# Deformable samples of a fused two-layer block: windows of 16 by 8 against two 8 by 8 patches on the halves of the array

## The chip, the cores and the metric

The kernel runs on one core of one Trainium2 chip, in float32 throughout, as one launch. The metric is device time in microseconds of that core. Five engines work side by side, each in its own order: TensorE (PE, its weight loads PEld), VectorE (DVE), ScalarE (ACT), GpSimd (POOL) and SyncE (SP), which here only issues transfers. Semaphores tie them together. Transfers run on 16 DMA engines.

## The reference, cut to what matters

Two layers act on x of 32 images, 128 channels, 32 by 32 points; each adds its result to its input, after a group norm of it. Layer 0 is a long convolution over the 1,024 points in 1,024 inner channels, with a GLU, a layer norm and a decoder. Layer 1 is a deformable depthwise convolution with 64 taps (8 by 8), and it is the one that the change touches:

```python
off = depthwise_conv3x3(x, offset_w) + offset_b      # 2 * 64 channels: dx, dy of each tap
for tap in range(64):                                # at each of the 32*32 points
    ix = (gx + kx[tap] + off[tap, 0]) * W / (W - 1) - 0.5
    iy = (gy + ky[tap] + off[tap, 1]) * H / (H - 1) - 0.5
    s = bilinear(x, iy, ix)                          # 4 neighbours, zero outside the image
    acc += s * weight[:, tap]
out = gelu(batch_norm(acc))
```

The offsets are the same for all channels, so a bilinear sample of all 128 channels is a matrix product: pixels of the image (rows) times weights of those pixels (columns). The weight of a pixel is a product of two hat functions, max(0, 1 - |ix - px|) and max(0, 1 - |iy - py|).

## The kernel before

The first stage (`ssm_kernel_table`, `ssm_convolution`) makes the convolution's result y for all images and leaves it in DRAM. `main_block` does the rest. Its order is written out by hand: Python generators yield the cost of what they have just issued, and `run_along` always advances the one that is least far along by its own total.

**first_part(b)** is the GLU of image b: two halves of 512 points, eight blocks m each, with eight products for the gate (L785), eight for the value (L808), one for the encoder (L824) and one for the decoder (L713), 128 rows by 512 columns; two more close a half. That is 292 products an image.

**second_part(b)** is layer 1 of image b. It runs beside `first_part(b + 2)`, so images 30 and 31 have no GLU beside them. The columns u = x + kx (39 of them) are grouped in 17 `PACKS`; a pack holds all (u, kx) pairs, called slots, whose samples lie in one window 8 pixels wide: 8 to 16 slots a pack, 254 in all. A pack is worked in four pieces of two ky each. A piece has 128 rows, the pixels of a window of 16 rows by 8, and a column for each slot, ky and output row y, up to 1,024. The y of a column decides in which of three windows (`YWINDOWS`, rows 0, 8 or 16 on) its sample lies, so a piece is three products (L1119), with `rows_of` giving the stretches of y. Each is scaled from PSUM by the tap's weight into `prod` (L1122, DVE). GpSimd adds the piece's two ky (L1139) and then adds them to the accumulator, u by u (L1144).

The moving operand of those products is made of two tables in DRAM for each image, `hat_d0` of 8 x hats and `hat_d1` of 16 y hats. For each piece `load_hat` loads them with repeats, the x hats into `ds` and the y hats into `dhy` (L1057, SyncE), and `weights(k)` multiplies the one by the other on DVE (L1076). `ds` has SB = 5 buffers and is loaded five pieces ahead; `dhy` has HB = 4 and is loaded four pieces ahead of its multiplication. A load is split into one for each run of neighbouring slots: one for most packs, two or four for the packs at the image's edges (25 runs a piece index over all packs, so 200 loads an image). The window of pixels comes with three loads of 128 runs of 512 bytes for each new x0 (L1090). In images 30 and 31 (`ALONE`) a quarter of `ds` is loaded and copied on (L1068).

**prepare(b + 1)** runs inside `second_part(b)`, as steps with due times on a scale of 204 an image: group norm, nine tap operations for the offsets, the transposed image to DRAM, then the positions `rel` (L934, L945), a `spread` of them to `rel_d` in DRAM with 16 copies of 256 runs of 128 bytes (L952), a `gather` back into two tiles (L966), and 24 hats: two ScalarE operations of 624 columns (L981, L982) and a write of 312 KB (L983) each, in two buffers. Image 0 is prepared in `opening`, beside `first_part(1)`:

```python
run_along((first_part(1), FIRST), (opening(), 90.0))
...
run_along(
    (first_part(b + 2, last=(b + 2 == B - 1)), FIRST),
    (second_part(b, steps), SECOND),
)
```

SyncE issues, in one order, the loads of `ds`, `dhy`, windows, y and u and the copies of `spread`; the writes of hats go out on ScalarE's queue. In the built program each of these transfers also waits for the one eight before it, since they share eight semaphores in turn. `deformable_redo` behind it repeats an image with a general method if its largest offset passes a bound (`BOUND_X`, `BOUND_Y`).

Of the kernel before, what the change touches and what calls it, by code (L numbers as in the profile page):

```python
# [515 lines left out]
KY2 = 2  # L516
SLOT = KY2 * H
PIECES = 8 // KY2
NPIECE = NU * 8 * SLOT
NCOL = PIECES * NPIECE  # L520
# [8 lines left out]
YWINDOWS = (0, 8, 16)  # L529
BOUND_X, BOUND_Y = 2.45, 3.25  # L530
# [9 lines left out]
def rows_of(piece):  # L540

    a, b = 15 - KY2 * piece, 23 - KY2 * piece
    return (0, a), (a, b - a), (b, H - b)
# [30 lines left out]
def main_block(nc, tc, const, ins, x, u_d, y_d, x1_d, out, offmax):  # L574
# [18 lines left out]
    ALONE = B - 2  # L593
    SB, HB = 5, 4
    ctx = ExitStack()
    with ctx:
# [5 lines left out]
        one, two, three = pool("mb1", 1), pool("mb2", 2), pool("mb3", 3)  # L602
        spool, hypool, hatpool = pool("mbs", SB), pool("mbh", HB), pool("mbq", 2)
        ppool = pool("mbp", 3)
# [34 lines left out]
        minus = constant("minus", [P, 16])  # L639
# [32 lines left out]
        rel_d = []  # L672
        zero = hatpool.tile([P, HSUB], F32, tag="hat", name="zero")
        nc.gpsimd.memset(zero, 0.0)
        for i in range(2):
            t = dram1.tile([2, NCOL], F32, tag=f"rel_d{i}", name=f"rel_d{i}")
            flat = t.rearrange("a (p l) -> (a p) l", p=P // 2)
            n = 2 * NCOL // P
            for lo in range(0, n, HSUB):
                w = min(HSUB, n - lo)  # L680
                nc.sync.dma_start(flat[:, lo : lo + w], zero[:, :w])
            rel_d.append(t)

# [177 lines left out]
        def prepare(b):  # L861
# [85 lines left out]
            def spread(a):  # L947
                def run():
                    for ky in range(8):

                        g = a * 8 + ky
                        nc.sync.dma_start(  # L952
                            at(
                                rel_d[b % 2],
                                a * NCOL + ky // KY2 * NPIECE + 7 * SLOT + ky % KY2 * H,
                                [[7 * SLOT, 8], [8 * SLOT, W], [1, H]],
                            ),
                            st["rel"][g * 8 : (g + 1) * 8],
                        )

                return run

            def gather(a):
                def run():
                    t = st["t", a] = one.tile([P, HSUB], F32, tag=f"rel{a}", name=f"dr_{b}_{a}")
                    nc.sync.dma_start(  # L966
                        t, at(rel_d[b % 2], a * NCOL, [[HSUB, P], [1, HSUB]])
# [4 lines left out]
            def hat(a, k):  # L972


                def run():
                    if k == 0:
                        st[f"h{a}"] = dram.tile(
                            [(8, 16)[a], NCOL], F32, tag=f"hat_d{a}", name=f"dhat_{b}_{a}"
# [5 lines left out]
                        at(st[f"h{a}"], k * NCOL, [[HSUB, P], [1, HSUB]]), t  # L984
# [4 lines left out]
            hats = [hat(0, k) for k in range(8)] + [hat(1, k) for k in range(16)]  # L989

            def turn(n):


                def run():
# [7 lines left out]
                    if n == 1:  # L1002
# [3 lines left out]
                        )  # L1006

                return run

            def ready():  # L1010
                images[b] = st["vt_d"], [st["h0"], st["h1"]]
# [5 lines left out]
                (71, largest), (74, across), (79, down), (81, spread(0)), (82, spread(1)),  # L1017
                (89, gather(0)), (90, gather(1)),
                *((96 + 82 * i // len(hats), step) for i, step in enumerate(hats)),
# [24 lines left out]
        def load_hat(k, a):  # L1044
# [4 lines left out]
            hats = images[b][1]  # L1049
            if a == 0:  # L1050
                t = s_of[k] = spool.tile([P, 16, KY2, H], F32, tag="s", name=f"ds_{k}")
            else:
                t = hy_of[k] = hypool.tile([P, 16, KY2, H], F32, tag="hy", name=f"dhy_{k}")
            rows = 4 if a == 0 and b >= ALONE else 16
            for first, slot, m in runs_of(n):
                dims = [[[0, rows], [NCOL, 8]], [[NCOL, rows], [0, 8]]][a]
                nc.sync.dma_start(  # L1057
                    t[: rows * 8, slot : slot + m],
                    at(hats[a], i * NPIECE + first * SLOT, [*dims, [1, m * SLOT]]),
                )  # L1060

        def spread_fine(k):

            if k >= len(pieces) or pieces[k][0] < ALONE:
                return
            m = slots_of(pieces[k][1])
            for n in (32, 64):
                nc.scalar.copy(s_of[k][n : 2 * n, :m], s_of[k][:n, :m])  # L1068
# [10 lines left out]
        def windows(b, n):  # L1079
# [4 lines left out]
            if b == B or (n > 0 and PACKS[n - 1][0] == x0):  # L1084
                return
            t = xw_of[b, x0] = three.tile(
                [P, len(YWINDOWS), C], F32, tag="xw", name=f"dxw_{b}_{x0}"
            )
            for j, y0 in enumerate(YWINDOWS):
                nc.sync.dma_start(  # L1090
                    t[:, j, :],
                    at(images[b][0], (y0 * W + x0) * C, [[W * C, 16], [C, 8], [1, C]]),
                )

        def second_part(b, steps):
# [6 lines left out]
            for n in range(NP):  # L1102
# [3 lines left out]
                windows(b, n + 1)  # L1106
                for i in range(PIECES):
                    k = (b * NP + n) * PIECES + i
                    s = s_of.pop(k)
                    w = wk[:, table_of[n] : table_of[n] + m, KY2 * i : KY2 * (i + 1)]  # L1110
                    prod = ppool.tile([P, 16, KY2, H], F32, tag="prod", name=f"dp_{k}")
                    for j, (y0, ny) in enumerate(rows_of(i)):
                        while steps and steps[0][0] <= 3 * (PIECES * n + i) + j:
                            steps.pop(0)[1]()
                        ps = psam.tile([P, 512], F32, tag="sam", name=f"dps_{k}_{j}")
                        ps = ps[:, : m * KY2 * ny].rearrange(
                            "p (s k y) -> p s k y", s=m, k=KY2
                        )
                        nc.tensor.matmul(  # L1119
                            ps, xw[:, j, :], s[:, :m, :, y0 : y0 + ny], start=True, stop=True  # L1120
                        )
                        nc.vector.tensor_mul(  # L1122
                            prod[:, :m, :, y0 : y0 + ny],
                            ps,
# [221 lines left out]
```

## Time and profile before

| | us |
|---|---|
| median of 3 runs (lowest, highest) | 13420.71 (13418.3, 13433.87) |
| the profiled execution | 13421.61 |
| its span, first to last instruction | 13419.9 |
| first memset of the accumulator (L1101), image 0 | 1827.2 |
| the same, image 30 | 12880.3 |
| the same, image 31 | 13164.7 |

The stage up to about 1,280 us is the long convolution. From there to 1,827 the GLU of images 0 and 1 runs; then 30 periods of one image's samples beside another's GLU; then two images of samples alone. A profile's group line reads: line, engine, operation, tiles written <- read, sizes and count, then busy us and mean ns of one, then how long the engine had idled ahead of such instructions and on whom. A float32 product appears as two PE records, each with a weight load (PEld); a record's end is modelled and overlaps the next one's start, so the cadence is read from start to start.

### The profile page before, as it was taken

What the parts mean: (1) busy time and instruction counts of PE and PEld (TensorE: products, weight loads), DVE (VectorE), ACT (ScalarE), POOL (GpSimd) and SP (SyncE); (2) the same over time, 40 slices, a digit from 0 to 9 for tenths busy, and PEclk for the clock granted to TensorE, in tenths of its full rate; (3) what the DMA queues carried; (4) which work ended last, traced back from release to release, by engine and by line L of the source; (5) the groups of instructions that cost most, each with busy time, mean ns of one, the idle gap of its engine ahead of it and who ended that gap; (6) DMA issues with size and microseconds to landing.
All of it is one profiled execution on the core that took longest, in us unless ns stands there. A gap on an engine that the chain in (4) does not pass through costs nothing.

```text
span 13419.9 us, 133500 instructions
## 1 busy us (share of the span) xinstructions
PE 12998.3 (97%) x40482; PEld 7208.8 (54%) x40482; DVE 8388.1 (63%) x12173; ACT 3279.7 (24%) x4767; POOL 9064.3 (68%) x8871
## 2 busy tenths in 40 slices
PE   7998999999999999999999999999999999999975
PEld 7998445555555555555555555555555555555533
DVE  5554146666666666666666666666666666666677
ACT  4433122222222212112222222211122222221245
POOL 2554147777777777777677777777777777777778
PEclk8999999999999999999999999999999999999988
DMA  7998068888888888888888888888888888888866
GB/s 232 274 284 267 19 172 235 240 235 236 232 230 240 236 228 228 233 231 239 237 237 232 229 239 239 231 225 232 231 240 236 236 232 231 236 240 232 232 194 174
DMA packets 1721768, 3055.43 MB, mean 228 GB/s; under 512 B 445523, under 2 KB 1024467, under 8 KB 1720019
## 3 DMA queue, kind: packets, MB, share of 16 engines
q1 hardware_dynamic: 1508434, 2591.60, 72.0%
q10 hardware_dynamic: 163456, 320.92, 6.6%
q0 software_dynamic: 49152, 134.28, 3.3%
q8 instruction: 328, 5.37, 0.2%
q14 instruction: 398, 3.25, 0.1%
HBM read 2580.03 MB, written 466.06 MB: 227 GB/s over the span
## 4 chain that ended last, share of the span: by engine, by line
PE 86%; DMA 7%; DVE 2%; ACT 2%; issue 1%; POOL 1%; SPq 1%; ACTq 0%; DVEq 0%; POOLq 0%
PE gpg L785 24%; PE gpv L808 24%; PE dps L1119 23%; PE psy L320 5%; DMA ds<-dhat 4%; PE gph L824 3%; PE gpo L713 3%; PE psz L237 3%; DMA dhat<-dh 1%; DVE ds L1076 1%; DMA dhy<-dhat 1%; ACT ds L1068 1%; SPq L1057 0%; DMA u<-u_d 0%; DVE dp L1122 0%
## 5 line engine op out<-in xcount | busy, mean ns | idle before, releaser
L1122 DVE TENSOR_TENSOR dp<-dps,k_weight_slots 128x256 f32<-128x256 f32 (+17 forms) x6528 | 3085.4, 483 | 3084.2 <-PE dps L1119 2908.7
L1119 PE MATMUL dps<-ds,dxw 128*128 128x256 f32 (+18 forms) x13056 | 4698.9, 447 | 227.5 <-DVE ds L1076 185.6
L1144 POOL TENSOR_TENSOR dacc<-dacc,dp 128x256 f32<-128x256 f32 (+3 forms) x4736 | 4403.9, 930 | 398.3 <-DVE dp L1139 28.5
L1119 PEld LDWEIGHTS dps<-ds,dxw 128*128 128x128 f32 x13056 | 2468.8, 192 | 3213.9 <-issue 2543.1
L785 PE MATMUL gpg<-gy,g_w_glu 128*128 128x512 f32 x8192 | 3986.4, 593 | 22.9 <-DMA gy<-y_d 18.2
L808 PE MATMUL gpv<-gy,g_w_glu 128*128 128x512 f32 x8192 | 3974.7, 592 | 0.0
L1139 POOL TENSOR_TENSOR dp<-dp 128x448 f32<-128x448 f32 (+2 forms) x2142 | 2671.9, 1247 | 1898.1 <-DVE dp L1122 1895.4
L1076 DVE TENSOR_TENSOR ds<-ds,dhy 128x1024 f32<-128x1024 f32 (+3 forms) x2176 | 3163.4, 1454 | 783.3 <-DMA ds<-dhat 675.5
L785 PEld LDWEIGHTS gpg<-gy,g_w_glu 128*128 128x128 f32 x8192 | 1544.5, 190 | 1237.0 <-issue 968.4
L808 PEld LDWEIGHTS gpv<-gy,g_w_glu 128*128 128x128 f32 x8192 | 1548.9, 189 | 1157.9 <-issue 915.1
L846 POOL TENSOR_TENSOR gs<-gs,gq 128x512 f32<-128x512 f32 x448 | 633.0, 1413 | 1348.2 <-ACT gq L845 1348.2
L845 ACT ACTIVATE gq<-gr 128x512 f32<-128x512 f32 x448 | 282.2, 630 | 4665.5 <-DVE gr L837 4603.9
L357 POOL DMA_DIRECT2D y_d<-yo x1024 | 589.5, 583 | 694.1 <-ACT yo L344 624.6
L792 ACT ACTIVATE gs<-gpg,k_b_glu 128x512 f32<-128x512 f32 x512 | 351.8, 687 | 2494.1 <-PE gpg L785 2378.0
L981 ACT ACTIVATE dh<-dr,k_minus 128x624 f32<-128x624 f32 x768 | 621.7, 809 | 654.7 <-DMA dhat<-dh 574.2
L320 PE MATMUL psy<-toe,z 128*128 128x192 f32 x4096 | 668.0, 326 | 7.4 <-DVE z L242 5.5
L320 PEld LDWEIGHTS psy<-toe,z 128*128 128x128 f32 x4096 | 663.0, 196 | 11.6 <-DVE z L242 6.8
L816 DVE SCALAR_TENSOR_TENSOR gs<-gpv,k_b_glu,gs 128x512 f32<-128x512 f32 x512 | 379.9, 742 | 437.2 <-PE gpv L808 436.8
L982 ACT ACTIVATE dh<-dh,one 128x624 f32<-128x624 f32 x768 | 626.2, 815 | 25.0
L715 POOL TENSOR_TENSOR gs<-gs,gr 128x512 f32<-128x512 f32 x448 | 631.7, 1410 | 0.0
L824 PE MATMUL gph<-gu,k_W_enc 128*128 128x512 f32 x1024 | 525.9, 595 | 30.1 <-DVE gs L816 30.1
L335 DVE TENSOR_TENSOR psy<-psy,t 128x256 f32<-128x256 f32 (+2 forms) x768 | 333.7, 434 | 346.1 <-ACT t L328 329.3
(163 smaller groups left out, 5810.3 us busy)
## 6 DMA issues: line engine op xcount, KB each, us to landing
dhy<-dhat SPq DMA_DIRECT2D x1536, 512.0 KB
ds<-dhat SPq DMA_DIRECT2D x1440, 512.0 KB
dhat<-dh ACTq DMA_DIRECT2D x768, 312.0 KB
y_d<-yo POOLq DMA_DIRECT2D x1024, 128.0 KB, 4.2
gy<-y_d SPq DMA_DIRECT2D x512, 256.0 KB
u<-u_d SPq DMA_DIRECT2D x224, 512.0 KB
dxw<-dvt_d SPq DMA_DIRECT2D x1248, 64.0 KB
dhy<-dhat SPq DMA_DIRECT2D x256, 224.0 KB
```

Of the source, the lines that this page charges most:

```text
L320: nc.tensor.matmul(ps[:, c // 2, c % 2, :], rows[i][:, (g * CG + c0 + c) // 2, c % 2, :], toe[:, c0 + c, :], start=True, stop=True,)
L715: nc.gpsimd.tensor_add(sums[0], sums[0], r)
L785: nc.tensor.matmul(gate, w_glu[:, k, D + m * P : D + m * P + P], ys[k], start=(k == 0), stop=(k == KD - 1),)
L808: nc.tensor.matmul(val, w_glu[:, k, m * P : m * P + P], ys[k], start=(k == 0), stop=(k == KD - 1),)
L824: nc.tensor.matmul(h, w_enc[:, m * P : (m + 1) * P], u, start=True, stop=True)
L846: nc.gpsimd.tensor_add(sums[1], sums[1], sq)
L982: nc.scalar.activation(t, t, AF.Relu, scale=-1.0, bias=const["one"])
L1076: nc.vector.tensor_mul(s[:, :m], s[:, :m], hy[:, :m])
L1119: nc.tensor.matmul(ps, xw[:, j, :], s[:, :m, :, y0 : y0 + ny], start=True, stop=True)
L1122: nc.vector.tensor_mul(prod[:, :m, :, y0 : y0 + ny], ps, w[:, :, :, None].to_broadcast([P, m, KY2, ny]),)
L1139: adder.tensor_add(prod[:, :m, 0], prod[:, :m, 0], prod[:, :m, 1])
L1144: nc.gpsimd.tensor_add(to, to, prod[:, slot : slot + nj, 0])
```

## The change

A piece is now four products of 64 rows. The rows of the array are two sides of 64, each a patch of 8 by 8 pixels; the columns of a side are 32 cells a slot, up to 512. Side 0 has the low rows v = y + ky, side 1 the high ones. Pieces 1 to 3 have, on each side, four neighbouring v for all eight ky; piece 0 has the rest at the top and bottom. Each side needs two patches (`parts_of`), which start at even rows, so there are two products of 64 rows a side, issued side 0, side 1, side 0, side 1. The sides write two PSUM tiles.

- `ds` and `dhy` tiles are half as wide. `ds` is one load a run as before (16 rows, eight repeats); `dhy` is now two loads of 64 partitions a run, 8 repeats of 8 rows. There are 8 y hats instead of 16, so 16 hats in place of 24.
- Pieces 1 to 3 are scaled by one DVE operation a side, piece 0 by four a side (`blocks_of`): 238 an image in place of 204. They write runs of four (or one) y into `prods`, two tiles of one pack each, laid out by ky.
- GpSimd sums the eight ky of a pack at once (three operations) and then adds to the accumulator, once for each u and pack: 37 additions an image in place of 148.
- The positions go to `rel_n` with two copies (`lay`), and 56 copies from DRAM to DRAM (`spread`) bring them into the order of the cells: 12 of 64 by 39 runs of 4 numbers, 28 of 8 by 39 runs of 1 to 6, and 16 of 8 by 39 single numbers. They are due at 81 to 108, the gathers at 112 and 113, the hats from 118 to 178.
- Patches are laid out in DRAM by 16 copies (`window`), and a pack's patches then come with two loads of 64 partitions for each x0, in two buffers instead of three.
- The special case for the last two images is gone. `BOUND_Y` falls from 3.25 to 2.45.

```diff
-KY2 = 2
-SLOT = KY2 * H
-PIECES = 8 // KY2
-NPIECE = NU * 8 * SLOT
-NCOL = PIECES * NPIECE
+CELLS = 32
+PIECES = 4
+SIDE = PIECES * NU * 8 * CELLS
+NCOL = 2 * SIDE
...
+def parts_of(side, piece):
+
+    if piece == 0:
+        return ((0, 0, 28), (6, 28, 32)) if side == 0 else ((6, 4, 32), (0, 0, 4))
+    w = 2 * (piece - 1) + side
+    return (w, 0, 2), (w + 1, 2, 4)
...
+                def move(to, ky, y, dims):
+                    frm = a * ASTEP + LEAST - 7 * H + ky * KSTEP + y
+                    moves.append(lambda: nc.sync.dma_start(
+                        at(rel_d[b % 2], a * NCOL + to, [[d[1], d[0]] for d in dims]),
+                        at(rel_n[b % 2], frm, [[d[2], d[0]] for d in dims]),
+                    ))
+
+                us = (NU, 8 * CELLS, H)
+                js = (8, CELLS, jump)
+                for side in range(2):
+                    base = side * SIDE
+                    for piece in range(1, PIECES):
+                        move(
+                            base + piece * NU * 8 * CELLS, 0,
+                            FIRST_V[side] + 4 * (piece - 1),
+                            ((64, 4, KSTEP - 1), us, (4, 1, 1)),
                         )
+                    for ky, y, n, cell in edges_of(side):
+                        move(base + cell, ky, y, (js, us, (n, 1, 1)))
+                    for i in range(4):
+                        ky = 4 * side + i
+                        move(
+                            base + (28, 0)[side] + i, ky, 19 - ky, (js, us, (1, 1, 1))
+                        )
...
-                (71, largest), (74, across), (79, down), (81, spread(0)), (82, spread(1)),
-                (89, gather(0)), (90, gather(1)),
-                *((96 + 82 * i // len(hats), step) for i, step in enumerate(hats)),
+                *((54 + i, window(i // 8, i % 8)) for i in range(16)),
+                (68, largest), (70, across), (74, down), (76, lay(0)), (77, lay(1)),
+                *((81 + i // 2, step) for i, step in enumerate(moves)),
+                (112, gather(0)), (113, gather(1)),
+                *((118 + 60 * i // len(hats), step) for i, step in enumerate(hats)),
...
+                if a == 0:
+                    nc.sync.dma_start(
+                        to, at(src, frm, [[SIDE, 16], [0, 8], [1, m * CELLS]])
+                    )
+                else:
+                    for side in range(2):
+                        nc.sync.dma_start(
+                            to[side * 64 : side * 64 + 64],
+                            at(
+                                src, frm + side * 8 * SIDE,
+                                [[0, 8], [SIDE, 8], [1, m * CELLS]],
+                            ),
+                        )
...
+                    for part in range(2):
+                        for side in range(2):
+                            half = slice(64 * side, 64 * side + 64)
+                            w, lo, hi = parts_of(side, i)[part]
+                            to, frm = ps[side], s[half, :m]
...
+                            nc.tensor.matmul(
+                                to[..., lo:hi], xw[half, w, :], frm[..., lo:hi],
+                                start=True, stop=True,
+                            )
+                    yield measure(m)
...
+                    due(1)
+                    scale(0)
+                    yield measure(m)
+                    due(2)
+                    scale(1)
+                    weights(k + 2)
+                    yield measure(m)
                     load_hat(k + SB, 0)
...
+                nc.gpsimd.tensor_add(rows(2, 2, 2), rows(2, 2, 2), rows(0, 6, 2))
+                nc.gpsimd.tensor_add(rows(2, 1, 1), rows(2, 1, 1), rows(4, 1, 1))
+                total = prod[:, 2 * KS : 2 * KS + m * H]
+                nc.gpsimd.tensor_add(total, total, prod[:, 3 * KS : 3 * KS + m * H])
```

In the changed kernel the products stand at L1224, the copies from DRAM to DRAM at L1002, the loads of `ds` at L1144 and of `dhy` at L1149.

## The prediction

> **What bounds the kernel now.** I read the page's busy shares and chain first, then the sums by stretch, then TensorE's and SyncE's order of time in single stretches.
>
> ```profile
> PE 12998.3 (97%) x40482; PEld 7208.8 (54%) x40482; DVE 8388.1 (63%) x12173; ACT 3279.7 (24%) x4767; POOL 9064.3 (68%) x8871
> PE 86%; DMA 7%; DVE 2%; ACT 2%; issue 1%; POOL 1%; SPq 1%; ACTq 0%; DVEq 0%; POOLq 0%
> ```
>
> ```profile
> 1835.00:12865.00 11030.00, 10963.39 (x30084) 5628.83 (x30083) 7142.79 (x10036) 2309.68 (x3061) 7950.49 (x7363) 1.00 0.86 233
> 12880.00:13164.00 284.00, 172.54 (x420) 91.36 (x420) 216.93 (x310) 181.13 (x195) 214.27 (x202) 0.79 0.65 189
> 13165.00:13420.00 255.00, 148.94 (x404) 79.83 (x404) 198.22 (x294) 134.12 (x135) 214.20 (x201) 0.85 0.62 175
> ```
>
> The columns are stretch, length, then busy time of PE, PEld, DVE, ACT and POOL, clock, DMA share, GB/s. The first row holds 30 images: each runs its samples beside another image's GLU (`first_part`). TensorE is busy 99% of it and nothing else over 72% (POOL), but the DMA engines stand at 0.86. The last two rows are images 30 and 31, which have no GLU beside them; there TensorE is not the bound. The accumulator's memsets (L1101) start at 1827.2 and, 30 images later, at 12880.3: 368.4 us an image.
>
> ```profile
> 6003.22 0.97 PE L1119 MATMUL dps<-ds,dxw 128*128 128x480 f32 x2
> 6004.02 1.88 PE L808 MATMUL gpv<-gy,g_w_glu 128*128 128x512 f32 x4
> 6005.74 0.97 PE L1119 MATMUL dps<-ds,dxw 128*128 128x480 f32 x2
> 6006.55 1.88 PE L808 MATMUL gpv<-gy,g_w_glu 128*128 128x512 f32 x4
> 6008.26 0.62 PE L1119 MATMUL dps<-ds,dxw 128*128 128x256 f32 x2
> ```
>
> Each product is two records. From start to start, two GLU products take 1.72 us, so 0.86 each (1.68 ns a column), and 480 sample columns take 0.81. An image has 292 GLU products (251 us) and 254 slots x 8 x 32 = 65,024 sample columns: 109 us, plus 204 products' small extra of 0.03 = 115. With 2 us for transposes and statistics the sum is 368: TensorE's order explains the period with nothing left over.
>
> **Part 1, TensorE.** 204 products of 128 rows become 272 of 64 rows with the same columns in all. If the halves do not work at the same time, that is 109 + 272 x 0.03 = 117 us, no gain. If they do, the order decides: side 0, side 1, side 0, side 1, each with two records, and the second record of a product needs the half that the first one holds. So side 1's first record runs beside side 0's second, and eight record lengths become five: 109 x 5/8 = 68, plus 5 for small extras = 73. Weight loads keep pace: in the first stage 368 records of 128 columns, each with a load ahead, take 41.50 us, 113 ns each; eight make 0.9 us a piece, under five records' 1.0.
>
> ```profile
> 284.70 41.50 PE psz L237 x368
> ```
>
> No row shows the array going from whole to halves. It may cost nothing; or the pipeline empties, at most the tail of a record, 593 - 430 = 163 ns. I take the tail, since it is what a wait for the last column would expose: 136 changes x 0.16 = 22 us. TensorE needs 251 + 2 + 73 + 22 = 348 us an image (326 without the changes; 392 if the halves take turns). The Trainium skill, TensorEngine Tiling (Array Packing), Key Properties, says that tiles run products in parallel and that changing the tiling mode drains TensorE. No run here shows either half of that; by its first half alone the image needs 326, by both 348.
>
> **Part 2, what gets lighter, off the path.** DVE is at 7142.79 / 30 = 238 us an image, POOL at 265.
>
> ```profile
> L1122 DVE TENSOR_TENSOR dp<-dps,k_weight_slots 128x256 f32<-128x256 f32 (+17 forms) x6528 | 3085.4, 483 | 3084.2 <-PE dps L1119 2908.7
> L1076 DVE TENSOR_TENSOR ds<-ds,dhy 128x1024 f32<-128x1024 f32 (+3 forms) x2176 | 3163.4, 1454 | 783.3 <-DMA ds<-dhat 675.5
> L1139 POOL TENSOR_TENSOR dp<-dp 128x448 f32<-128x448 f32 (+2 forms) x2142 | 2671.9, 1247 | 1898.1 <-DVE dp L1122 1895.4
> L1144 POOL TENSOR_TENSOR dacc<-dacc,dp 128x256 f32<-128x256 f32 (+3 forms) x4736 | 4403.9, 930 | 398.3 <-DVE dp L1139 28.5
> ```
>
> The weights' product halves to 128x512 (0.84 us for that form): 99 to 54 us. The scaling has 238 operations for 204 on the same columns; forms of 480 (655 ns) and 256 (415) give 1.07 ns a column and 0.14 fixed: 96 to 103. POOL's sums of ky rise from 83 to about 142 (7 m x 32 elements a pack at 2.5 ns), its additions to the accumulator fall from 148 to 37, 138 to 34. DVE 200, POOL 220 of some 370: hidden by TensorE. Strided runs of four could slow DVE; it has 150 us of cover. Loads of ds and dhy halve in bytes.
>
> **Part 3, SyncE and its transfers.** This decides. Loads go from 200 to 300 an image (each hy load is now two), window loads from 39 to 26, and the 16 copies of rel_d become 2 to rel_n, 16 of windows and **56 copies from DRAM to DRAM**: 12 of 2,496 runs of 16 bytes and 44 of 312 runs of 4 to 24 bytes. All are due in 28 of the image's 204 steps.
>
> ```profile
> 1707.14 9.11 SPq L952 DMA_DIRECT2D rel_d<-drel  x16
> 1789.50 10.13 SPq L1057 DMA_DIRECT2D dhy<-dhat  x16
> ```
>
> Both stretches are nearly quiet otherwise. Sixteen copies of 256 runs of 128 bytes take SyncE 9.11 us, 0.57 each, 2.2 ns a run; a load of 128 rows takes 0.63. In the trace's semaphore records a load gives 16 updates, but a rel_d copy, whose outermost count is 8, gives 9; I read that as eight engines instead of sixteen. A 312-run copy (outermost 8 too) then costs 0.6, a 2,496-run copy (outermost 64, all engines, so 1.1 ns a run) 2.8. Ends: 0.6 for either, if size is free, 34 us in all; or the average packet of the main queue, 72.0% of 16 engines x 13,420 us / 1,508,434 packets = 102 ns. An engine of the lower eight gets 12 x 156 + 44 x 39 = 3,588 runs: 366 us. I take the rel_d row, the nearest in size and kind: 44 x 0.6 + 12 x 2.8 = **60 us**. Below 34 nothing can go: each copy is an issue. The Trainium skill, DMA: Bandwidth & Descriptors, Specifications, says that transfers under 512 B are read, modified and written. Runs of 128 B already fall under it, and no run here shows runs of 4 to 24; it gives no price, so only the chance of the dear case leans on it.
>
> Behind each copy on SyncE stand the loads of ds and dhy. In 28/204 x 348 = 48 us SyncE must issue 60 us of copies, 9.4 pieces x 3 loads x 0.63 = 18, and 4 of others: 82. A ds load goes out five pieces ahead, 25 us; landing (the chain shows mostly 7.5 to 13) and the product on DVE leave 15. So 82 - 48 - 15 = **19 us** in which DVE waits for ds, and behind it both the samples and the GLU (its PSUM is emptied by DVE). At the image's edges the packs of four and two runs need 144 loads x 0.63 = 91 us in 16 pieces of about 4.7: less the 15, with 3 for others, 4 us more. An image: 348 + 19 + 4 = 371, +2.6.
>
> On the lower eight engines the two hy halves (outermost 8) and ds make 24 rows a piece, at 0.1 us 163 an image, with 60 of copies and some 75 of the rest about 300 of 371: close behind, so no large gain can come even if SyncE is quick.
>
> **Part 4, once.** In the built order 34 of image 0's 56 copies (6 large), both gathers and all 16 hats stand behind the last GLU work of `first_part(1)`; before, only 2 of 24 hats did. Copies 28 x 0.6 + 6 x 2.8 = 34, gathers 6, hats 16 x 2.3 (0.81 + 0.82 on ACT and a write into one of two buffers) = 37, first loads 18: +95, uncovered. Clearing rel_n: +4. Image 31 alone: 330 issues x 0.62 = 205 for 255, -50; image 30, with copies, stays at 284.
>
> **Sum** against the profiled execution's own 13,421.61 (the median of three is 13,420.71, the same): 13,422 + 30 x 2.6 + 95 + 4 - 50 = 13,549, so **13,550**.
>
> **Rivals.** (a) *Faster: a copy costs only its issue*, 0.6 whatever its size, so SyncE's window work is 56 us against 48 + 15 and no stall remains. For: issues of loads do not grow with their bytes. Against: the first two of the 16 rel_d copies issue in 0.3 us, the rest in about 0.6, as if held by their runs. Then 352 an image: 13,422 - 30 x 16.4 + 49 = 12,980; with changes of the array free as well, 330 and 12,320. It decides once a large copy costs under 2.4 us, where the image is at the old 368. (b) *Halves take turns*: the change does not do what it says. 392 + 13 + 4 = 409: 13,422 + 30 x 40.6 + 49 = 14,690. (c) *Tiny runs are dear*, at 50 ns, half the average packet: 179 us on the lower engines, with 22 of the rest against 63: stall 138, 490 an image, 17,100; at the full 102 ns, 22,700. It begins to decide above 17 ns a run, where the copies take 60 us.
>
> **Chances.** Forecast (13,300 to 14,000) 0.36; (a) 0.32; (b) 0.14; (c) 0.18. Range 12,500 to 15,600: it cuts (a)'s cheapest end and most of (c). The likeliest cases have both signs; the forecast's own range is 13,300 to 14,000. A measurement here tells 0.2%, 27 us. Faster: all of (a) and 0.01 of the forecast, 0.33; same 0.05; slower 0.30 + 0.14 + 0.18 = 0.62.
>
> **What would show it.** L1224's records of the two sides start within a few ns of each other in part (halves work together) or each waits for the other's end (b). The gap from the last sample record to the next GLU record shows the change's price. SyncE's L1002 rows show a copy's price, 0.6 or 2.8. DVE's idle time ahead of the weights' product, released by ds, is 19 us an image or not. A period of the memset near 371 confirms the sum; near 330 the stall is wrong, near 490 the run's price is.

## The result, and the profile after

| | before | after |
|---|---|---|
| median, us | 13423.69 | **15383.85** (15355.62 to 15387.74, 4 runs each) |
| ratio | | **1.1455**, 95% interval 1.1435 to 1.1475 |
| span of the profiled execution, us | 13419.9 | 15353.9 |
| image 0, memset to memset of `dacc` | 377.4 | 549.6 |
| an image in the steady state (images 1 to 29) | 368.1 | 425.0 |
| image 30 / image 31 to the end | 284.4 / 255.2 | 373.4 / 272.8 |

(The median before is that of the three runs on record and one more, taken beside those of after; the spans and images are from the two profiled executions.) The changed kernel is 14.6% slower; 1.0% was forecast. The spans differ by 1,934 us: the start 7, image 0 172, the next 29 images 1,648, image 30 89, image 31 18.

The page after, its busy shares and the two lines of its chain:

```profile
PE 12804.7 (83%) x44834; PEld 6423.9 (42%) x44834; DVE 7648.1 (50%) x13227; ACT 2597.5 (17%) x3983; POOL 7419.6 (48%) x4811
PE 61%; SPq 19%; DMA 13%; DVE 3%; issue 2%; ACT 1%; POOL 0%; ACTq 0%; DVEq 0%; POOLq 0%
PE gpg L822 19%; PE gpv L845 18%; PE dps L1224 12%; SPq L1002 9%; SPq L1149 6%; DMA ds<-dhat 5%; PE psy L320 4%; DMA rel_d<-rel_n 4%; SPq L1144 3%; PE psz L237 3%; PE gpo L750 3%; PE gph L861 2%; DVE prod L1238 1%; DMA dr<-rel_d 1%; DVE ds L1163 1%
```

SyncE's queue had 1% of the chain before and has 19% now; its own line of the copies (L1002) is the largest entry that is not a product. The three stretches that answer to the rows of before (the columns are the same):

```profile
1834.00:14707.00 12873.00, 10825.41 (x34228) 4847.48 (x34228) 6477.25 (x11091) 1949.08 (x2615) 6397.13 (x3542) 0.90 0.62 131
14708.00:15081.00 373.00, 140.00 (x546) 87.43 (x542) 180.58 (x316) 33.48 (x43) 173.91 (x90) 0.52 0.63 131
15082.00:15354.00 272.00, 136.44 (x530) 85.52 (x530) 172.32 (x303) 1.36 (x2) 171.70 (x90) 0.54 0.58 145
```

TensorE is busy 84% of the 30 images, where it was 99%; its clock is 0.90 where it was 1.00, and the DMA engines moved less (0.62, 131 GB/s against 0.86, 233). No engine and no bandwidth is at its limit. The idle time has one place. Stretches of one image (6,643.7 to 7,066.3):

```profile
6764.00:6804.00 40.00, 38.23 (x126) 17.15 (x122) 18.02 (x35) 2.00 (x3) 24.90 (x14) 0.96 0.59 73
6804.00:6844.00 40.00, 10.54 (x28) 3.79 (x26) 3.60 (x8) 0.63 (x1) 1.91 (x2) 0.63 0.74 73
6844.00:6884.00 40.00, 23.01 (x57) 10.15 (x58) 7.41 (x18) 1.90 (x3) 6.27 (x5) 0.76 0.60 52
6884.00:6944.00 60.00, 58.13 (x180) 26.10 (x177) 39.95 (x65) 21.36 (x27) 33.34 (x17) 0.92 0.82 225
7034.00:7066.00 32.00, 20.56 (x50) 8.80 (x49) 8.60 (x19) 2.60 (x3) 14.90 (x9) 0.73 0.44 120
```

From 6,804 to 6,884 TensorE works 34 of 80 us, at a clock of 0.63 and 0.76; at the image edge (7,034 on) 21 of 32. Elsewhere it is full. What SyncE does just ahead of the first hole, in order of time (start, length, what):

```profile
6770.42 14.81 SPq L1002 DMA_DIRECT2D rel_d<-rel_n  x6
6785.34 3.47 SPq L1149 DMA_DIRECT2D dhy<-dhat  x2
6788.90 0.54 SPq L1144 DMA_DIRECT2D ds<-dhat  x1
6789.48 1.23 SPq L1175 DMA_DIRECT2D dxw<-dxw_d  x2
6790.76 4.07 SPq L1002 DMA_DIRECT2D rel_d<-rel_n  x6
6794.93 1.23 SPq L1149 DMA_DIRECT2D dhy<-dhat  x2
6796.27 0.54 SPq L1144 DMA_DIRECT2D ds<-dhat  x1
```

Six copies hold SyncE for 14.81 us, and one piece's three loads follow them; another six, another piece. A piece in the full stretches takes about 5 us. Until 6,888 SyncE is occupied with 56 copies and the loads between them. The loads themselves land much as ever: `ds` 4.7 us after its issue began (median of nine) in this window, 5.7 in the 120 us ahead of it. Over images 1 to 29, nine tenths of the full `ds` loads (128 rows of 2 KB) land within 7.0 us of the end of their issue, and without the copies (the first run below) within 7.1. They are late because they are issued late. SyncE does not wait for earlier copies either: the waits that end with the landing of a copy add up to 251 us in the whole run, 8 an image, where issuing the copies takes 77. Two groups of the page name who waits (busy, mean ns, idle before and its releaser):

```profile
L1224 PE MATMUL dps<-ds,dxw 64*128 64x256 f32 (+9 forms) x17408 | 2790.3, 429 | 1727.0 <-DVE ds L1163 1408.1
L1163 DVE TENSOR_TENSOR ds<-ds,dhy 128x512 f32<-128x512 f32 (+3 forms) x2176 | 2277.1, 1046 | 3906.8 <-DMA ds<-dhat 3450.2
```

VectorE waits 3,450 us for `ds`, before 675.5; the samples wait for VectorE.

### The profile page after: what moved, and what is told of

Its sections match the earlier page's. It is cut to its first block, busy times and chain, and to the rows that moved or that the text cites. A ratio compares the mean times of both kernels' runs of the same rounds, so it can differ in the third digit from the quotient of the medians.

```text
span 15353.9 us, 145811 instructions
## 1 busy us (share of the span) xinstructions
PE 12804.7 (83%) x44834; PEld 6423.9 (42%) x44834; DVE 7648.1 (50%) x13227; ACT 2597.5 (17%) x3983; POOL 7419.6 (48%) x4811
## 4 chain that ended last, share of the span: by engine, by line
PE 61%; SPq 19%; DMA 13%; DVE 3%; issue 2%; ACT 1%; POOL 0%; ACTq 0%; DVEq 0%; POOLq 0%
PE gpg L822 19%; PE gpv L845 18%; PE dps L1224 12%; SPq L1002 9%; SPq L1149 6%; DMA ds<-dhat 5%; PE psy L320 4%; DMA rel_d<-rel_n 4%; SPq L1144 3%; PE psz L237 3%; PE gpo L750 3%; PE gph L861 2%; DVE prod L1238 1%; DMA dr<-rel_d 1%; DVE ds L1163 1%
## 5 line engine op out<-in xcount | busy, mean ns | idle before, releaser
L822 PE MATMUL gpg<-gy,g_w_glu 128*128 128x512 f32 x8192 | 4174.6, 650 | 657.0 <-DMA gy<-y_d 656.6
L1262 POOL TENSOR_TENSOR prod<-prod 128x2048 f32<-128x2048 f32 (+3 forms) x544 | 2428.4, 4464 | 3807.6 <-DVE prod L1238 3807.6
L1224 PE MATMUL dps<-ds,dxw 64*128 64x256 f32 (+9 forms) x17408 | 2790.3, 429 | 1727.0 <-DVE ds L1163 1408.1
L1163 DVE TENSOR_TENSOR ds<-ds,dhy 128x512 f32<-128x512 f32 (+3 forms) x2176 | 2277.1, 1046 | 3906.8 <-DMA ds<-dhat 3450.2
L1238 DVE TENSOR_TENSOR prod<-dps,k_weight_slots 128x512 f32<-128x512 f32 (+9 forms) x7616 | 3115.9, 448 | 2219.9 <-PE dps L1224 2101.7
L845 PE MATMUL gpv<-gy,g_w_glu 128*128 128x512 f32 x8192 | 3856.6, 610 | 0.0
L1224 PEld LDWEIGHTS dps<-ds,dxw 64*128 64x128 f32 x17408 | 1702.6, 203 | 3752.4 <-issue 3212.8
L1263 POOL TENSOR_TENSOR prod<-prod 128x1024 f32<-128x1024 f32 (+3 forms) x544 | 1353.2, 2487 | 42.7
L829 ACT ACTIVATE gs<-gpg,k_b_glu 128x512 f32<-128x512 f32 x512 | 351.8, 687 | 3722.5 <-PE gpg L822 3697.3
L1270 POOL TENSOR_TENSOR dacc<-dacc,prod 128x256 f32<-128x256 f32 (+6 forms) x1184 | 807.9, 682 | 92.8
L1265 POOL TENSOR_TENSOR prod<-prod 128x512 f32<-128x512 f32 (+3 forms) x544 | 748.5, 1376 | 42.7
```

The source lines that it names most:

```text
L822: nc.tensor.matmul(gate, w_glu[:, k, D + m * P : D + m * P + P], ys[k], start=(k == 0), stop=(k == KD - 1),)
L845: nc.tensor.matmul(val, w_glu[:, k, m * P : m * P + P], ys[k], start=(k == 0), stop=(k == KD - 1),)
L1163: nc.vector.tensor_mul(s[:, :m], s[:, :m], hy[:, :m])
L1224: nc.tensor.matmul(to[..., lo:hi], xw[half, w, :], frm[..., lo:hi], start=True, stop=True,)
L1238: nc.vector.tensor_mul(cell(ky, y, rows, skew, run), ps[side][:, :, at_cell : at_cell + rows * run].rearrange("p s (k v) -> p s k v", k=rows),
L1262: nc.gpsimd.tensor_add(rows(2, 2, 2), rows(2, 2, 2), rows(0, 6, 2))
```

## The experiments

A *hold* is the length of an issue on the engine that makes it. Times without an interval are single executions; the four executions of a kernel that was run more often lie within 0.3%. Landing times are those of the full `ds` loads of images 1 to 29, from the end of their issue, unless it says otherwise.

Two theories were on record. **A, the issuer's order:** an engine that issues a copy of many short runs is held until it has been taken over, and what stands behind it on that engine comes late. **B, the DMA engines:** the short runs occupy the 16 DMA engines, and everybody's transfers land late, whoever issues. Both price the short runs; they differ on what moving the copies to another queue would do.

**No copies.** `moves = spread(0) + spread(1)` became `moves = []`: the positions are not brought into the order of the cells.

> The changed kernel without its 56 copies from DRAM to DRAM; it leaves out the layout of the positions, so the hats are those of zero positions. Theory A (the loads stand behind the copies in SyncE's order): the stall at the copies goes, the one at the image's edge stays, so the period falls from 425 to about 350 us and the run to about 13,050. Theory C (the halved loads themselves, the hy halves on eight engines or the 64-row products, are what is slow): the period stays at 400 or more, the run above 14,600.

Measured 13,095 us; 356 us an image, image 0 378.9. The copies cost 2,290 us, more than the whole loss, and C is out. It says nothing between A and B.

**Copies on ScalarE.**

```diff
-                    moves.append(lambda: nc.sync.dma_start(
+                    moves.append(lambda: nc.scalar.dma_start(
```

> The changed kernel with the 56 copies issued on ScalarE's queue instead of SyncE's; nothing else moves. Theory A (order on SyncE): the loads no longer wait for the copies' issue, the period falls to 340 to 370 us, the run to 12,800 to 13,700, if ScalarE's own wait does not delay the GLU. Theory B (the short runs fill the 16 DMA engines, whoever issues them): the loads still come late, the period stays above 405, the run above 14,700.

Measured 14,969 us, 412 an image: read by its time alone, B. But ScalarE has other work, and its order of time shows where that went (the bracket is idle time and releaser):

```profile
6666.68 0.63 ACT L882 ACTIVATE gq<-gr 128x512 f32<-128x512 f32 x1 [19.71 <-DMA rel_d<-rel_n]
6667.09 20.98 ACTq L1002 DMA_DIRECT2D rel_d<-rel_n  x12
6688.17 0.69 ACT L829 ACTIVATE gs<-gpg,k_b_glu 128x512 f32<-128x512 f32 x1 [20.86 <-DMA rel_d<-rel_n]
6688.19 12.41 ACTq L1002 DMA_DIRECT2D rel_d<-rel_n  x5
```

Twelve copies hold ScalarE for 20.98 us, and the GLU's activation (L829) stands behind them. Four such waits in and around the 100 us from 6,654 on add up to 101 us. The loads on SyncE land in 5.4 us on average in that image, as without copies (5.2), so on average the short runs did not delay them. The hold went to another engine with work on the path, which A had named as its condition. But SyncE was not free either: here the copies share the eight semaphores with SyncE's loads, and these waited 1,320 us (`dhy`) and 447 us (`ds`) in the run for a copy to land, 55 us an image; in the changed kernel no such wait stands in the list. So this run moved the price in two ways, and its time settles nothing between A and B.

**Copies one a step, opening longer.** One copy a step from 80 to 136 instead of two, each half's gather and hats behind its own copies, and `(opening(), 160.0)` for 90.0.

> The changed kernel with one copy a step instead of two (steps 80 to 136 of 204), the second gather at 141, the hats behind their own gather, ready at 184; and in the opening the generator's total is 160 instead of 90, so that image 0 is prepared before the GLU of image 1 ends. Theory A: SyncE has 3 x 1.4 + 3 x 0.62 + 0.6 = 6.7 us a piece against 4.95 of TensorE over 19 pieces, 33 us too much, 15 covered: stall about 18 in place of 66, period about 375, and the opening saves about 100: 13,800. Theory B: the engines' work spreads over twice the time, no stall is left at the copies, period about 350, 13,050.

Measured 14,933 us, which neither expected. Image 0 is 425.7 from a memset 53 us later: 71 us are saved there, 12 of them in every image. The steady image is 412.6. L1002 fell from 77 to 54 us an image, but a full `dhy` load (64 rows of 2 KB, 96 an image) now takes SyncE 820 ns to issue, against 653 in the changed kernel and 600 without copies. All of SyncE's issues together take 305 us an image, 299 in the changed kernel: the loads between the copies took over what L1002 lost. So the hold is no property of the copy instruction; it falls on what comes next in the queue.

**No large copies.** `for piece in range(1, PIECES)` became `range(0)`: the twelve copies of 2,496 runs are left out, and with them most of the order.

> The changed kernel without the 12 large copies (2,496 runs each), the 44 small ones kept; it leaves out the layout of the positions for pieces 1 to 3. Theory A with the price per run: SyncE keeps 44 x 0.64 = 28 us of copies and 22 of others in 48, covered, so the period is that without any copy, about 350, the run about 13,100. If instead each copy costs its issue and the number of copies counts, most of the stall stays: 44 of 56, period about 405, 14,700.

Measured 13,547 us, 368 an image, nearer to A with a price per run (13,100) than to a price per copy (14,700). The large copies cost 1,837 us, the 44 small ones 451 that A had as covered.

**Large copies in another order.** `((64, 4, KSTEP - 1), us, (4, 1, 1))` became `(us, (64, 4, KSTEP - 1), (4, 1, 1))`.

> The twelve large copies of an image move the same 2,496 runs of 16 bytes each, but in another order: 64 runs that land side by side, then the next column, where before 39 runs landed 1 KB apart, then the next of 64. The theory: SyncE is held while it issues a copy of many runs (29.3 us an image for the twelve large ones, 77 us for all 56), the hold goes by the number of runs and not by where they land, and the loads of weights behind it come late: 15,250 to 15,500 us. The rival, that runs landing 1 KB apart are what is slow: 13,600 to 14,500 us, with the large copies' issue falling towards 0.6 us.

Measured 16,822 us: slower still, which neither expected. L1002 has 15% of the chain and 110 us an image; a large copy lands 16.7 us after the end of its issue, 11.2 before (means). The semaphore records show a part of the reason: these copies, whose outermost count is 39, give 14 updates where those of 64 gave 16. The Trainium skill, DMA: Bandwidth & Descriptors, Why a DMA increments its semaphore by 16 and not by 1, says that a copy runs on the largest number of engines up to 16 that divides its outermost counts, and that the issuer makes up the missing increments in one write. For 39 that is 13 engines; 13 and one write are the 14 updates. An engine then has 192 runs instead of 156, 1.23 times as many; the landing takes 1.49 times as long, so a part stays open. The holds of all copies grew 1.43 times with the same number of runs, so the number alone does not set them, as the theory had it; they went with how long the copies took to land. Runs that land side by side gained nothing that shows.

**Long runs.** The large copies keep their bytes and waits and move whole kilobytes (`((NU, 8 * CELLS, 256), (256, 1, 1))`, which end up as 16 runs of 2,496 bytes); the order of the positions is lost.

> The twelve large copies of an image stay, with the same bytes and the same waits, but each moves 39 runs of 1 KB where there were 2,496 of 16 bytes; this leaves out the order of the positions that these copies made. The theory (the hold goes by the number of runs): the large copies issue in about 0.6 us each, 7 us an image, the small ones as they do without the large ones (32 us), so 39 us of holds against 77: 13,600 to 13,900 us, a little over the 13,547 us without large copies. The rival, that a copy from DRAM to DRAM of this size, or the wait for its landing, is what costs: 15,100 to 15,500 us.

Measured 13,703 us, as the theory had it. A large copy issues in 0.59 us, and the small ones fall too: those with 24-byte runs from 2.8 to 0.67 us on average. In the changed kernel they paid for the large ones ahead of them. This is the run that shows the cause: as many copies, bytes and waits on the same queue, and 53 of the 69 us go. These five kernels with the copies on SyncE and at the same steps line up:

| SyncE's L1002, us an image | 0 | 32 (no large) | 37 (long runs) | 77 (after) | 110 (other order) |
|---|---|---|---|---|---|
| us an image | 356 | 368 | 372 | 425 | 471 |

From 37 us on each further microsecond of these holds goes with 1.3 to 1.4 us of time.

**Copies on GpSimd.** `nc.gpsimd.dma_start`, at the old steps.

> All 56 copies are issued by GpSimd instead of SyncE. The theory (the price is that SyncE's loads stand behind the copies; issued by ScalarE, the GLU's activations stood behind them for 101 us in one window): SyncE's loads pass freely, and GpSimd, busy for 7,430 us of the span, has room for some 60 us more an image: 13,000 to 13,500 us if its issue costs no more than SyncE's 1.4 us. The rival, that the short runs slow the DMA engines for every queue: 14,500 to 15,400 us, with weights landing later than the 5 us after issue that they take now. If GpSimd's own issue of 2,496 runs takes far longer than SyncE's, its products come late instead, and the time says nothing for either.

Measured 14,999 us, 414 an image, where the rival would have it. The group of the copies:

```profile
L1002 POOL DMA_DIRECT2D rel_d<-rel_n x1792 | 1497.7, 839 | 1024.8 <-DMA rel_d<-rel_n 879.9 <-DMA rel_n<-drel 129.1 <-issue 13.6
```

GpSimd needs 47 us an image to issue them and waits 880 us in the run for earlier copies to land (its copies take eight semaphores of their own in turn), with its sums behind. `ds` also lands later now: nine tenths within 10.0 us, in the changed kernel 7.0. And SyncE's loads do not pass freely: its `gather` (L1029) waits for the copies to land, 1,175 us in the run (66 in the changed kernel), and every load behind it waits too. That is 37 us an image, where the image is 58 above the one without copies. Three things are mixed here, and the time says nothing for either theory alone.

**Second half's `dhy` on ScalarE.** `(nc.sync, nc.scalar)[side].dma_start(...)` in `load_hat`; copies stay on SyncE.

> The dhy loads of the second half are issued by ScalarE; the copies stay on SyncE. The theory that SyncE's queue is what is late: 12 issues a piece at the packs of four runs become 8, the stall at the image edge (some 18 us an image without any copies) goes, and the copies hold up fewer loads: 14,500 to 15,000 us. The rival, that the edge stalls for another reason and ScalarE's activations now wait behind loads: 15,200 us or more.

Measured 14,625 us, 402 an image, as the theory had it. With 100 of 300 loads an image off SyncE, 23 us of an image go. The next run shows that 15 of them are the edge, which stalls without copies too; some 8 are left for the copies.

**No copies and `dhy` on ScalarE**, to price the edge alone; the order of positions is left out.

> No copies at all, which leaves out the laying out of the positions, and the second half's dhy loads on ScalarE. It prices the image edge by itself: without copies the time was 13,095 us with 18 us an image of idle TensorE at the edge. The theory (SyncE's 12 issues a piece at the packs of four runs): 12,400 to 12,700 us. The rival, that the edge stalls for another reason: 13,000 us or more.

Measured 12,624 us, 471 less than without copies alone. At the edge of the changed kernel SyncE issues eight `dhy` (4.94 us) and four `ds` (2.45) for each piece of a pack with four runs, with hardly a wait in between, so a piece takes 7.4 us. This kernel shows what TensorE alone needs, 341 us an image at a clock of 1.00:

```profile
1840.00:12093.00 10253.00, 10144.26 (x34221) 4577.65 (x34222) 6511.86 (x11086) 1930.71 (x2582) 6458.84 (x3540) 1.00 0.63 162
```

**Everything moved.** The copies one a step, large ones three or four small ones apart, `dhy` split, opening 160; the copies all on GpSimd, or the large ones on GpSimd and the small ones on SyncE, or all on SyncE.

> Three things together: the 56 copies on GpSimd, one a step with the large ones three or four small ones apart, so that GpSimd need not wait for a landing before the next; the second half's dhy loads on ScalarE; and 160 units for the first image's copies in place of 90. The theory (whoever issues the copies is held; GpSimd was held by its issue for 47 us an image and by waits for landings for 30 more; SyncE was late at the image edge besides): about the 13,095 us without copies, less the edge's stall of some 18 us an image (550 us), plus what GpSimd's 47 us cost: 12,600 to 13,200 us. The rival, that GpSimd's products come late behind its copies whatever their spacing: 13,400 us or more.

> As the run with all copies on GpSimd, spread out, but the 44 small copies on SyncE and only the twelve large ones on GpSimd. The theory: GpSimd's holds fall from 47 to 15 us an image, SyncE's are 32 us, which cost some 12 us an image when they stood alone in a crowd and less spread out: 12,600 to 13,200 us. The rival, that the 16-byte runs slow every queue: above 13,800 us.

> The same spacing, the dhy loads of the second half on ScalarE and the 160 units, but all copies on SyncE. The theory (SyncE's order): the spread copies alone gave 14,933 us, and the loads on ScalarE took 760 us off the changed kernel: 14,000 to 14,400 us, a thousand and more above the runs with copies on GpSimd. The rival, that the spacing and not the queue is what helps: within 200 us of those.

Measured 13,670 us (1.0184 of before, 1.0167 to 1.0201), 13,842 (1.0315, 1.0298 to 1.0332) and 14,259. The last has the time that A gave, but it is 590 and 420 us above the other two where a thousand and more was expected. The first two are 470 and 640 us above their ranges, in the ranges of their rivals. With the copies on GpSimd, and the gathers later, SyncE hardly stands behind them (L1029 waits 137 us in the run), and still VectorE waits:

```profile
L1169 DVE TENSOR_TENSOR ds<-ds,dhy 128x512 f32<-128x512 f32 (+3 forms) x2176 | 2880.2, 1324 | 1655.9 <-DMA ds<-dhat 1329.4
```

Nine tenths of the `ds` loads land within 13.5 us now, 7.6 without copies. DMA has 21% of the chain, GpSimd 2%, so GpSimd's products, the rival, are not what is late. That is B, but not "whoever issues": it goes by the queue. Full `ds` loads issued while a large copy was on its way took 13.2 us on average in the run with all copies on GpSimd (the others 5.3) and 6.5 in the one with all on SyncE at the same spacing (5.3); with the copies on ScalarE it was 7.5 (5.2). The packet records differ too: on SyncE's queue each run of 16 bytes is a packet of its own, of 16 ns on average in the run with all copies on SyncE; on GpSimd's the runs stand in packets of up to 1,024 bytes, and those of 1,024 took 416 ns. That these long packets are what the loads wait for was not tried.

**The same with long runs** (large copies as in the run above, on GpSimd): is it the runs or the work of GpSimd?

> As the run with all copies spread out on GpSimd, but the twelve large copies move 39 runs of 1 KB in place of 2,496 of 16 bytes; this leaves out the order of positions that they made. The theory (with the loads free, what is left of the copies' price is the DMA engines' work on the short runs, behind which loads land late): 12,700 to 12,950 us, and nine tenths of the ds loads land within 8 us of issue again. The rival (GpSimd's issue holds its products up): 13,450 to 13,700 us.

Measured 12,787 us. Nine tenths land within 8.3 us (8 expected), VectorE's wait for `ds` is 367.7 us, although GpSimd still issues 56 copies an image. The runs, then: 883 us of the 1,046 that the copies cost there. (GpSimd's issuing falls with them, from 47 to 39 us an image; but GpSimd had 2% of the chain ahead of this.)

**More time for the runs, and one load more ahead.** Three steps for two copies, from step 71 on; then also `SB, HB = 6, 4`.

> As the run with all copies spread out on GpSimd, but three steps for every two copies, over 84 steps in place of 57, begun nine steps earlier, with the second half's hats ending seven steps later. The theory (loads land late because the short runs crowd the DMA engines for a time): a third to a half of what is left of the copies' price goes, 13,150 to 13,450 us. The rival (each run costs the same wherever it stands): 13,550 to 13,750 us.

> As the run with the copies on GpSimd and spread over 84 steps, with six buffers for ds in place of five, so that a ds load has one piece (some 5 us) more from issue to need. The theory (ds lands up to 13 us after issue where five buffers give less): 13,100 to 13,400 us, below the kernel before. The rival (dhy, or GpSimd's products, are late instead): 13,420 to 13,500 us.

Measured 13,471 us (1.0043 of before, 1.0026 to 1.0060) and **13,342 us (0.9943, 0.9926 to 0.9959)**. The first is 21 us above the range of the theory: the spread took 199 of the 1,046 us, a fifth and not a third. The second hit: VectorE's wait for `ds` fell from 1,462 to 513 us. It is the only version here with the whole work that beats the kernel before, by 0.6%.

```profile
L1169 DVE TENSOR_TENSOR ds<-ds,dhy 128x512 f32<-128x512 f32 (+3 forms) x2176 | 2918.0, 1341 | 807.4 <-DMA ds<-dhat 513.1
```

## Why the prediction was wrong

The direction, the bound and the place were right; one term was mis-sized by more than three times, and it decides.

| us an image | forecast | measured | from |
|---|---|---|---|
| TensorE | 348 | 341 | no copies, `dhy` split |
| image edge | 4 | 15 | 356 - 341, all that the split of `dhy` gave |
| stall by the copies | 19 | 69 | 425 - 356 |
| sum | 371 | 425 | |

**Part 1, TensorE: right in sum, wrong inside.** The halves work together, better than forecast: records of side 0 and side 1 start 7 ns apart (6,911.071 and 6,911.078 us, then .404 and .411, .631 and .637, .857 and .864), so a piece takes four record lengths and not five. (In the kernel without copies and with `dhy` split, the two records of every such pair in images 1 to 29 start within 20 ns.) One visit to the halves, with what stands ahead and behind, in TensorE's order of time:

```profile
6910.12 1.02 PE L861 MATMUL gph<-gu,k_W_enc 128*128 128x512 f32 x2
6911.07 1.18 PE L1224 MATMUL dps<-ds,dxw 64*128 64x256 f32 x8
6912.18 2.41 PE L822 MATMUL gpg<-gy,g_w_glu 128*128 128x512 f32 x5
```

Eight records of 256 columns take 1.11 us from start to start; four lengths at the 0.226 us of the last pair are 0.90, and the first pair takes 0.33. Going to halves and back cost more than the 0.16 taken: of 341 us the GLU and others have 253 and four lengths of 109 / 8 have 54.5, which leaves 33.5 for 68 visits, 0.49 each with small extras, against 22 + 5 forecast. The starts of the records in that kernel say nearly the same: the last GLU record ahead of a visit takes 523 ns to the next start and the first one behind it 533, against 429 elsewhere, and the visit itself 1.07 us where four lengths are 0.80; 0.46 in all, 0.20 of it at the two changes. The two errors, one length too many and too little for the visits, nearly cancel: that the sum came out is luck. The Trainium skill, TensorEngine Tiling (Array Packing), Key Properties, says that a change of the tiling mode drains TensorE; the longer records on both sides agree with it, and no run here shows the drain by itself. Rival (b), halves in turn, is out.

**Part 2: right in what matters.** VectorE's scaling takes 97 us an image (103 forecast) and GpSimd's sums 142 (142). The weights' product takes 71 (54 forecast; 1,046 ns each against 840). VectorE is busy 216 us an image (200) and GpSimd 213 (220), both under TensorE.

**Part 3 failed**, at the step "44 x 0.6 + 12 x 2.8 = 60 us". The copies hold SyncE for 77 us. The large ones were nearly right (29 us for twelve, 2.4 each); the small ones were not (48 us for 44, 1.1 each), because a hold falls on whatever comes next in a queue that is filled. The price had been taken from a stretch where 16 copies of 256 runs met a nearly empty queue. The rest of the window work, forecast at 22, took 42 in the image shown: 31 for the issue of the loads in between, the rest in waits and gaps. SyncE is in the window until 6,888, 117 us after it entered at 6,770, 75 of it in copies. By the forecast's own rule, 117 less 48 and 15 of cover, that makes 54 where 19 was forecast. The remainder, up to 69, was not in the reasoning. One part may be that the cover of 15 us had to serve the copies and the loads behind them; that was not tried. Another is that TensorE ran slower in and behind its idle time (0.63, 0.76 and 0.92 in the rows above, 1.00 from 6,644 to 6,764). The 30 images have 34,228 TensorE records in either kernel, within ten; they take 10,825 us here and 10,144 without copies and edge stall. That is 681 us, a quarter of the 2,620 between those two stretches. It is a reading of busy times; no experiment shows the clock's part by itself.

The same step had **the edge** at 4 us: it set 144 loads against 15 us of lead for 16 pieces as a whole. The packs of four runs alone need 12 issues, 7.4 us, a piece, and the lead is spent in the first few. Measured 15.

Rival (c) had the runs dear, at 50 ns of a DMA engine's time each, with loads landing late. In the changed kernel the packets of 16 bytes took 19 ns on average (median 9), near the 17 where it begins to decide, and the loads land on time; loads land clearly late only with the copies on GpSimd (883 us). Rival (a) is out: with long runs the same 56 copies cost 53 us an image less.

**Part 4.** Forecast were +95 for the opening and +4 ahead of it. Image 0 shows 172 against before; 57 of that every image has, so 115 and 7 ahead are left. Without copies 14 are left: image 0 takes 378.9, 23 more than the images behind it, and 9 more before. The copies that stand behind the GLU there:

```profile
1828.46 47.38 SPq L1002 DMA_DIRECT2D rel_d<-rel_n  x34
1875.88 2.56 SPq L1029 DMA_DIRECT2D dr<-rel_d  x2
```

They hold SyncE for 47.4 us, 34 forecast: the same mis-sized price, without cover. Image 30 was said to stay at 284; without copies it does (288.6), with them it takes 373. Image 31 was to gain 50 and lost 18. The forecast bound it by SyncE's issues, but with a third of its loads on ScalarE (no copies, `dhy` split) it still takes 262 us, 12,360.1 to 12,622.5; in the changed kernel no engine is busy for more than 172 of its 272, and what bounds it was not tried.

## What to carry to other kernels

Price a transfer by its contiguous runs, by how many engines share them and by what stands behind it on the engine that issues it; a queue that is filled charges the next instruction, so a price read in an empty stretch is a lower end. Moving such copies to another queue only helps if nothing on the path stands behind them there, and if the first queue waits for them neither through shared semaphores nor through whatever reads their result. Then look again: issued by GpSimd, the short runs delayed SyncE's loads, and spacing and one more buffer of lead are what helped. A long window of holds cost more than its length here, 1.3 to 1.4 times.

## What the runs showed of the hardware

- Records of two 64-row halves started 7 ns apart (median) and ran side by side throughout; a visit to the halves cost about 0.5 us between whole-array products.
- A copy of 2,496 runs of 16 bytes landed 11.2 us after its issue with 16 semaphore updates and 16.7 with 14; as 16 runs of 2,496 bytes it landed in 2.8.
- The same runs of 16 bytes were packets of 16 bytes on SyncE's queue and of up to 1,024 on GpSimd's; a full `ds` load issued while such a copy was on its way landed in 6.5 us and in 13.2.
- A hold showed up on the next instructions of the queue: copies with 24-byte runs issued in 2.8 us behind large copies, in 0.67 behind long-run ones.
- VectorE's product of the weights (L1163, then L1169) took 1,054 ns without copies (`dhy` split) and 1,260 to 1,341 ns in the four kernels with all copies spread out on GpSimd, with short runs or long. Why was not tried.
